# Five due times moved in a two-layer graph attention kernel: a reciprocal and its fetch, one norm, one block turn

## The chip, the cores and the metric

The kernel runs on one core of a Trainium2 chip. The metric is the device time of one execution in microseconds (us). Five engines work beside each other, each through its own instructions in order: TensorE (PE, with its weight loads shown as PEld), VectorE (DVE), ScalarE (ACT), GpSimd (POOL), and SyncE (SP), which here only issues DMAs. POOL also issues some.

## The reference

Two layers of masked attention over 16 graphs of 1024 nodes with 256 features. Layer 0 has 4 heads of 64, layer 1 has 8 heads of 32 and biases. Cut to what matters (the second layer is the same with its own weights):

```python
h = jnp.maximum(_layernorm(x, axis=-1), 0.0)
q, k, v = heads(h @ Wq), heads(h @ Wk), heads(h @ Wv)
scores = q @ k.T * scale                      # per head, 1024 x 1024
scores = jnp.where(adj > 0, scores, -jnp.inf)
out = jax.nn.softmax(scores, axis=-1) @ v
x = x + concat(out) @ Wo.T + bo
```

## The kernel before

**Steps.** `layer_steps` cuts one layer of one batch into groups and steps. A group is one half of the queries (`qh`, 512 of them) with one half of the heads (`g`); each layer has four groups, in the order (qh 0, g 0), (0, 1), (1, 0), (1, 1). A group has 4 steps in layer 0 and 8 in layer 1. A step computes four score tiles of 128 x 512 on TensorE (`scores`, L539) into two pairs of banks out of a ring of three; DVE masks each pair (`exponentials`, L562), which frees its banks; ACT takes the exponential (L568). Two steps later (`LEAD`) `weigh` (L580) multiplies with the values. POOL and accumulating DMAs of POOL's queue (L695, L681) add up the exponentials, and `count` (L425) sums them over the partitions. Layer 0's steps run in pairs, and the scores of a pair need four pairs of banks, one more than the ring has.

**Rounds.** The list of steps alternates: the 16 steps of layer 0 of batch b+1, then the 32 steps of layer 1 of batch b, for b from 0 to 14. This text calls that round b, its layer 0 steps a+0 to a+15 and its layer 1 steps c+0 to c+31 (`a` and `c` in the code). c+32 is a+0 of the next round. Before round 0 stand 16 steps of layer 0 of batch 0, after round 14 the 32 steps of layer 1 of batch 15.

**Due times.** Everything else is written down by hand with `later(i, f, ...)`: at step i, after that step's scores, weighing and exponentials have been issued, call f. Entries of one step run in the order in which they were put down, except that functions with matmuls (`LARGE`) come last. Entries that the program's loop over b puts down (L899 to L944) are there before the first step runs, and so stand ahead of those that `end_group` adds while the steps run. In a pair of layer 0 steps the entries of both follow the exponentials of both; those of the even step come first, then `add_tiles`, then those of the odd one. The instructions go into each engine's queue in this order, which nothing reorders.

**End of a group** (`end_group`, L742). It is called two steps after the group's last step, and puts down, at distances `at`: `spread` (ACT copies the sums out of PSUM, L445; four SP DMAs spread them over the partitions, `sums<-s`, L458), `invert` (a DVE reciprocal, L466, and an SP DMA to DRAM, `vd<-vn`, L468), `fetch` (four SP DMAs that bring it back, repeated over the partitions, `inv<-vd`, L477), `normalize` (POOL, L485), and for g = 1 `end_half` (the product with Wo, L521, and DVE's addition to x, L526). For layer 1 the third group's entry (qh 1, g 0) is `(7, 9, 11, 14)`; the group ends at c+23 and is closed at c+25, so its spread is at c+32 = a+0 of the next round, its invert at a+2, its fetch at a+4 and its normalize at a+7. The fourth group has 4, 6, 7, 9, 11 from c+33: spread at a+5, invert at a+7, fetch at a+8, normalize at a+10, `end_half` at a+12.

**Masks.** `Mask.load` brings a part of adj by four SP DMAs (L152) into one buffer (`bufs=1`); `put` (ACT, L167) rewrites it, `flip` (DVE, L173) turns its blocks, `second` (ACT, L178) changes it for layer 1. In a round the loads of the batch after next stand at a+5, a+8, a+10, a+12, a+14, a+45, a+49 and a+51; the last two are a+1 and a+3 of the next round, and each put stands in the step of the following load, the last one at a+53, which is a+5 of the next round. So at a+5 the put of one batch's last part and the load of the next batch's first part stand in one step.

**Inputs.** `norms` puts down the stats (DVE, L198 and L199, with four small POOL operations) and the norm (ACT, L221, two of them for two row tiles) of half a batch, into one buffer `hn`. `block_inputs` puts down `turn_blocks` (DVE transposes 32 x 32 blocks of hn, L273), `put_blocks` (one SP DMA to DRAM, `turned<-hn`, L278), `place_blocks` (four SP DMAs back as `hT`, L285), and then the matmuls that make k, q and values. In layer 1 of round b that happens for layer 0 of batch b+2 (`other`), and from round 1 on for layer 1 of batch b (`mine`), whose first steps stand at the end of the round before, hence a - 27 and so on. a - 18 is c+14 of the round before.

Of the kernel before, what the change touches and what calls it, by code (L numbers as in the profile page):

```python
# [90 lines left out]
def fast_program(ctx, tc, a, w, loads, chk):  # L91
# [514 lines left out]
    class Stream:  # L606
# [12 lines left out]
        def later(self, i, f, *args):  # L619
            self.due.setdefault(i, []).append((f, args))  # L620
# [121 lines left out]
        def end_group(self, i, gr):  # L742

            if gr.hurry:
                for f in (gr.spread, gr.finish, gr.inp.test):
                    self.later(i, f)
                return

            if gr.layer == 0:
                if gr.g == 0:  # L750
                    gr.half.first = gr
                    return
                early = gr.inp.b == 0 and gr.qh
                self.later(i + (2 if early else 3), gr.count_added)
                at = (3, 4, 5, 7, 13) if gr.qh else (3, 5, 6, 7, 11)
                if gr.inp.b == B - 1 and gr.qh:
                    at = 3, 6, 7, 9, 13
                if gr.inp.b == 0:
                    at = (2, 3, 4, 5, 8) if gr.qh else (3, 5, 6, 7, 9)
            else:  # L760
                at = ((9, 11, 13, 19), (8, 12, 14, 17, 19), (7, 9, 11, 14), None)[2 * gr.qh + gr.g]
                if gr.pairs:
                    at = 2, 5, 6, 7, 9
                elif gr.last:
                    at = 4, 6, 7, 9, 11
            for k, f in zip(at, (gr.spread, gr.invert, gr.fetch, gr.normalize)):
                self.later(i + k, f)
            if gr.last:

                k = 7 if gr.layer or gr.inp.b == 0 else 25 if gr.inp.b == B - 1 else 37  # L770
                self.later(i + k, gr.inp.test)
            if gr.g == 1:
                self.later(i + at[4], gr.end_half)
# [82 lines left out]
    def norms(inp, half, *at, whole=False, bias=None):  # L856

        for k, i in enumerate(at):
            f, rest = (inp.norm, (whole,)) if k > 1 else (inp.stats, ())
            later(i, f, half, (2, 3) if k % 2 else (0, 1), *rest)  # L860
        later(at[3] + 1 if bias is None else bias, inp.add_bias, half)

    def half_inputs(inp, half, *at):

        for i, f in zip(at, (inp.turn, inp.k, inp.q, inp.values)):
            later(i, f, half)

    def block_inputs(inp, half, turn, put, place, *at):

        later(turn, inp.turn_blocks, half)  # L870
        later(put, inp.put_blocks, half)
        later(place, inp.place_blocks, half)
        parts = inp.k_part, inp.q_part, inp.values_part
        for i, f, part in zip(at, (inp.k, inp.q, inp.values), parts):
            if type(i) is tuple:
                for m in range(2):
                    later(i[m], part, half, m)
            else:
                later(i, f, half)
# [19 lines left out]
    for b in range(B - 1):  # L899
        mine, a, c = inputs[1][b], first[b + 1], second[b]  # L900
        if b == 0:

            norms(mine, 0, a + 4, a + 6, a + 7, a + 8, whole=True)
            half_inputs(mine, 0, a + 10, a + 12, a + 13, a + 14)
            norms(mine, 1, a + 10, a + 11, a + 12, a + 13, whole=True)
            half_inputs(mine, 1, a + 15, c, c + 6, c + 2)
        else:
            norms(mine, 0, a - 27, a - 26, a - 19, a - 17, bias=a)
            block_inputs(mine, 0, a - 14, a - 11, a - 5, a, a + 2, a + 8)
            norms(mine, 1, a - 14, a - 14, a - 8, a - 6, bias=a + 6)  # L910
            block_inputs(mine, 1, a, a + 6, a + 7, c, c + (6 if b + 2 < B else 10), c + 2)
        for i, u in zip((0, 2, 4, 6, 7, 9, 11, 13), range(NT)):
            later(a + i, masks[b].second, u)
        if b + 2 < B:
            other, mask = inputs[0][b + 2], masks[b + 2]
            later(a + 6, open_x, b + 2, 0)
            later(c, open_x, b + 2, 1)
            if b == 0:
                norms(other, 0, a + 12, a + 14, c, c + 1, bias=c + 34)
                block_inputs(other, 0, c + 2, c + 3, c + 4, (c + 8, c + 10), (c + 12, c + 16), c + 18)  # L920
                norms(other, 1, c + 3, c + 4, c + 6, c + 7, bias=c + 36)
                block_inputs(other, 1, c + 8, c + 9, c + 12, (c + 20, c + 22), c + 26, (c + 28, c + 30))
            else:
                norms(other, 0, a + 10, a + 12, a + 13, a + 15, bias=c + 34)
                block_inputs(other, 0, c, c + 1, c + 2, (c + 8, c + 10), (c + 12, c + 16), c + 18)
                norms(other, 1, c + 2, c + 4, c + 5, c + 6, bias=c + 36)
                block_inputs(other, 1, c + 7, c + 8, c + 12, (c + 20, c + 22), c + 26, (c + 28, c + 30))
            at = 5, 8, 10, 12, 14, 45, 49, 51, 53
            for t in range(NT):
                later(a + at[t], mask.load, t)  # L930
                later(a + at[t + 1], mask.put, t)
                later(a + at[t + 1] + (1 if t == 4 else 2), mask.flip, t)
        else:
            last, e = inputs[1][b + 1], c + 32
            later(c + 5, last.stats, 0)
            later(c + 10, last.norm, 0)
            later(c + 13, last.add_bias, 0)
            block_inputs(last, 0, c + 11, c + 12, c + 13, c + 18, c + 22, c + 26)
            later(c + 18, last.stats, 1)
            later(c + 22, last.norm, 1)  # L940
            later(c + 23, last.add_bias, 1)
            block_inputs(last, 1, c + 23, c + 24, c + 26, e, e + 10, e + 2)
            for i, u in zip((4, 10, 14, 26, 36, 40, 42, 44), range(NT)):
                later(c + i, masks[b + 1].second, u)  # L944
# [157 lines left out]
def kernel(  # L1102
# [28 lines left out]
    with ExitStack() as fast, tc.manual_schedule():  # L1131
        fast_program(fast, tc, a, w, loads, chk)
# [61 lines left out]
```

## Time and profile before

| what | value |
|---|---|
| median of 3 runs | 3083.88 us (3083.51 to 3085.02) |
| the profiled execution | 3083.88 us |
| its span, first to last instruction | 3082.1 us |
| granted TensorE clock | 0.999 |
| scores L539, on PE | 1089.9 us busy |
| weighing L580, on PE | 967.9 us busy |
| masking L562, on DVE | 1791.6 us busy, 1.215 us each |
| exponentials L568, on ACT | 1615.9 us busy, 1.056 us each |
| tile sums L695, on POOL | 1218.1 us busy, 2.472 us each |
| reciprocal L466, on DVE | 95 of them, 0.244 us each |
| block turn L273, on DVE | 58 of them, 1.239 us each |

Busy times are those of one engine, and the engines overlap. In the timeline, a row is one or several instructions of one line that follow each other: its start in us, its length, engine, line, operation, what it writes and reads, and how many; in brackets stands the idle time of the engine before it and what ended that. SPq rows are DMAs that SP issues: their length is the issuing alone, not the transfer. In the list of waits, a row names who waited for whom, the sum in us, how often, and the longest. An `x8` on a row of scores means the two passes of four matmuls, so one step of layer 1, and `x16` a pair of layer 0 steps.

### The profile page before, as it was taken

To read this page: it belongs to the slowest core of one execution; us is meant where nothing else is said; L and a number is where in the kernel's file an instruction comes from. 1 tells how busy PE (TensorE), PEld (TensorE's weight loads), DVE (VectorE), ACT (ScalarE), POOL (GpSimd) and SP (SyncE) were. 2 spreads that over 40 slices of the span, in tenths; PEclk is the share of its full clock that TensorE was granted. 3 is DMA by queue.
4 is the path that set the end of the run, shared out by engine and by line. 5 is a ranking of instruction groups with operands and counts; after the bars stand their busy time and mean duration, and the time that the engine had idled before them with its cause. 6 is when DMAs were issued, how large, how long until landed. Compare 5 with 4: busy or idle time off the path is not lost.

```text
span 3082.1 us, 46012 instructions
## 1 busy us (share of the span) xinstructions
PE 3061.3 (99%) x16678; PEld 1199.8 (39%) x16678; DVE 2464.4 (80%) x2712; ACT 2242.9 (73%) x2478; POOL 2462.1 (80%) x1584
## 2 busy tenths in 40 slices
PE   9999999999999999999999999999999999999998
PEld 4443433434334343343433334343343433434333
DVE  6778787887878878787887878878788787887877
ACT  5668777777777767777777777777777777776775
POOL 3578788787887878878788887888878778787886
PEclk9999999999999999999999999999999999999999
DMA  4226556464563645546456463654636546463431
GB/s 134 63 61 147 129 123 135 121 141 121 129 145 110 139 130 133 136 110 138 124 129 138 120 139 108 147 123 122 141 104 144 132 122 138 118 143 86 100 82 34
DMA packets 263548, 372.77 MB, mean 121 GB/s; under 512 B 58768, under 2 KB 218768, under 8 KB 242448
## 3 DMA queue, kind: packets, MB, share of 16 engines
q0 software_dynamic: 23472, 170.93, 28.2%
q1 hardware_dynamic: 239520, 198.56, 22.2%
q8 instruction: 133, 2.18, 0.3%
q14 instruction: 103, 0.84, 0.1%
q10 hardware_dynamic: 320, 0.26, 0.0%
HBM read 149.95 MB, written 47.96 MB: 64 GB/s over the span
## 4 chain that ended last, share of the span: by engine, by line
PE 92%; DVE 2%; DMA 2%; POOL 1%; issue 1%; SPq 1%; ACT 1%; DVEq 0%; ACTq 0%; POOLq 0%
PE ps L539 31%; PE po L580 28%; PE pq L307 10%; PE py L521 7%; PE pv L383 6%; PE pq L348 5%; PE pz L425 4%; PE pv L367 2%; DVE p L562 1%; DMA p<-p 1%; POOL p L695 1%; DMA sums<-s 0%; DMA inv<-vd 0%; ACT p L568 0%; SPq L458 0%
## 5 line engine op out<-in xcount | busy, mean ns | idle before, releaser
L562 DVE SCALAR_TENSOR_TENSOR p<-mask,ps 128x1024 f32<-128x1024 fp8e5 x1536 | 1791.6, 1215 | 346.0 <-PE ps L539 327.2
L568 ACT ACTIVATE p<-p 128x1024 f32<-128x1024 f32 x1536 | 1615.9, 1056 | 597.1 <-DVE p L562 535.4
L695 POOL TENSOR_TENSOR p<-p,p 128x1024 f32<-128x1024 f32 x510 | 1218.1, 2472 | 104.9 <-PE po L580 104.3
L539 PE MATMUL ps<-qT,kT 32*128 32x512 f32 (+1 forms) x6144 | 1089.9, 629 | 5.5 <-DVE p L562 3.5
L580 PE MATMUL po<-p,v 128*32 128x512 f32 (+1 forms) x6144 | 967.9, 599 | 0.4 <-ACT cat L437 0.4
L539 PEld LDWEIGHTS ps<-qT,kT 32*128 32x128 f32 (+1 forms) x6144 | 355.4, 184 | 640.2 <-DVE p L562 269.5
L580 PEld LDWEIGHTS po<-p,v 128*32 128x32 f32 (+1 forms) x6144 | 239.4, 118 | 669.7 <-issue 498.6
L593 POOL TENSOR_TENSOR p<-p 128x1024 f32<-128x1024 f32 x128 | 302.8, 2366 | 79.4 <-DVE p L592 74.1
L592 POOL TENSOR_TENSOR p<-p,p 128x1024 f32<-128x1024 f32 x64 | 151.2, 2363 | 157.3 <-DVE p L589 128.9
L485 POOL TENSOR_TENSOR cat<-cat,inv 128x512 f32<-128x512 f32 x127 | 175.2, 1383 | 77.7 <-DMA inv<-vd 76.5
L521 PE MATMUL py<-wo,cat 128*128 128x256 f32 x1008 | 234.4, 386 | 0.0
L521 PEld LDWEIGHTS py<-wo,cat 128*128 128x128 f32 x1008 | 186.3, 190 | 73.5 <-issue 16.7
L681 POOL DMA_DIRECT2D p<-p x163 | 144.8, 889 | 86.5 <-DMA p<-p 55.2
L383 PE MATMUL pv<-wv,hT 128*128 128x256 f32 x800 | 185.7, 385 | 0.0
L307 PE MATMUL pq<-hT,wq 128*128 128x512 f32 x400 | 184.8, 605 | 0.1
L167 ACT ACTIVATE mask<-adj,numbers 128x1024 fp8e5<-128x1024 int32 x128 | 145.9, 1140 | 45.0 <-DMA adj<-in_adj_dram 45.0
L383 PEld LDWEIGHTS pv<-wv,hT 128*128 128x128 f32 x800 | 148.0, 190 | 57.1 <-issue 25.2
L589 DVE TENSOR_TENSOR p<-p 128x1024 f32<-128x1024 f32 x128 | 166.9, 1304 | 0.0
L526 DVE TENSOR_TENSOR x<-py,x 128x1024 f32<-128x1024 f32 x63 | 77.1, 1224 | 109.1 <-PE py L521 109.1
L437 ACT COPY cat<-po 128x512 f32<-128x512 f32 x128 | 73.7, 576 | 118.5 <-PE py L521 96.6
L595 POOL TENSOR_TENSOR p<-p,p 128x1024 f32<-128x1024 f32 x64 | 151.9, 2373 | 5.0
L230 POOL TENSOR_TENSOR x<-x,bo 128x1024 f32<-128x1024 f32 x64 | 155.7, 2503 | 0.0
(71 smaller groups left out, 1961.2 us busy)
## 6 DMA issues: line engine op xcount, KB each, us to landing
p<-p POOLq DMA_DIRECT2D x163, 1024.0 KB, 7.9
adj<-in_adj_dram SPq DMA_DIRECT2D x512, 128.0 KB, 3.0
turned<-hn SPq DMA_DIRECT2D x58, 512.0 KB, 3.6
hT<-turned SPq DMA_DIRECT2D x232, 128.0 KB, 2.9
x<-in_x_dram SPq DMA_DIRECT2D x128, 128.0 KB, 3.0
inv<-vd SPq DMA_DIRECT2D x128, 128.0 KB, 3.0
inv<-vd SPq DMA_DIRECT2D x252, 64.0 KB, 2.5
out_dram<-x SPq DMA_DIRECT2D x124, 128.0 KB, 2.2
```

What stands on the lines that cost most here:

```text
L230: nc.gpsimd.tensor_add(rows, rows, w.bo[self.layer].unsqueeze(1).to_broadcast([P, 4, E]))
L307: nc.tensor.matmul(pq[:, m, :], wt[self.layer][:, c, ts(m, P)], self.hT[half][:, c, :], start=(c == 0), stop=(c == 1),)
L383: nc.tensor.matmul(pv[:, i, :], self.hT[half][:, c, ts(i, P)], w.v[self.layer][:, c, :], start=(c == 0), stop=(c == 1),)
L485: nc.gpsimd.tensor_mul(o, o, inv)
L521: nc.tensor.matmul(py[:, i, :], self.half.cat[:, c, ts(i, P)], w.o[self.layer][:, c, :], start=(c == 0), stop=(c == 1),)
L539: nc.tensor.matmul(st.ps[i // 2][:, i % 2, :], gr.inp.kT[r * D : (r + 1) * D, gr.g, ts(kt, P)], gr.inp.qT[gr.qh][r * D : (r + 1) * D, gr.g ...
L562: nc.vector.scalar_tensor_tensor(out=half, in0=gr.mask.m[gr.qh][:, kt // 4, :, kt % 4].unsqueeze(1).to_broadcast([P, 2, 512]), scalar=-EDG ...
L568: nc.scalar.activation(half, half, AF.Exp, scale=gr.scale)
L580: nc.tensor.matmul(gr.o[r * D : (r + 1) * D, :], gr.inp.v[:, kt, h * D : (h + 1) * D], st.halves[i // 2][:, i % 2, :], start=(kt == 0), st ...
L589: nc.vector.tensor_add(a, a, b)
L593: nc.gpsimd.tensor_add(a, a, b)
L695: nc.gpsimd.tensor_add(half, half, of)
```

## The change

Four lines of due times, in three places. In `end_group`, the third group of layer 1 has its invert two steps later and its fetch one step later. In the loop, the first of the two norms for the first half of the next layer 1 batch is one step later. And the second half of the batch after next has its block turn, its put and its place later: by two, two and one steps in rounds 1 to 13, by one each in round 0.

```diff
             else:
-                at = ((9, 11, 13, 19), (8, 12, 14, 17, 19), (7, 9, 11, 14), None)[2 * gr.qh + gr.g]
+                at = ((9, 11, 13, 19), (8, 12, 14, 17, 19), (7, 11, 12, 14), None)[2 * gr.qh + gr.g]
...
-            norms(mine, 0, a - 27, a - 26, a - 19, a - 17, bias=a)
+            norms(mine, 0, a - 27, a - 26, a - 18, a - 17, bias=a)
...
             if b == 0:
...
                 norms(other, 1, c + 3, c + 4, c + 6, c + 7, bias=c + 36)
-                block_inputs(other, 1, c + 8, c + 9, c + 12, (c + 20, c + 22), c + 26, (c + 28, c + 30))
+                block_inputs(other, 1, c + 9, c + 10, c + 13, (c + 20, c + 22), c + 26, (c + 28, c + 30))
             else:
...
                 norms(other, 1, c + 2, c + 4, c + 5, c + 6, bias=c + 36)
-                block_inputs(other, 1, c + 7, c + 8, c + 12, (c + 20, c + 22), c + 26, (c + 28, c + 30))
+                block_inputs(other, 1, c + 9, c + 10, c + 13, (c + 20, c + 22), c + 26, (c + 28, c + 30))
```

## The prediction

> **What bounds the kernel.** I read the page's busy times first, then the waits, then the timeline of one round, engine by engine. A round is the 48 steps that repeat: the layer 0 pairs a+0 to a+15 of one batch, then the layer 1 steps c+0 to c+31 of the batch before.
>
> ```profile
> PE 3061.3 (99%) x16678; PEld 1199.8 (39%) x16678; DVE 2464.4 (80%) x2712; ACT 2242.9 (73%) x2478; POOL 2462.1 (80%) x1584
> PEclk9999999999999999999999999999999999999999
> PE 92%; DVE 2%; DMA 2%; POOL 1%; issue 1%; SPq 1%; ACT 1%; DVEq 0%; ACTq 0%; POOLq 0%
> DVE vn L466 <- DMA sums<-s: 52.3, 27, 4.4
> ```
>
> TensorE (PE) is busy in all of the span and 92% of the chain that ended last is its own. So a microsecond on another engine counts only where TensorE then stands still. The change moves no matmul: stats, norms, block turns, puts, places, reciprocals and fetches are DVE, ACT, POOL and SP work. TensorE's own work therefore stays, and the answer is the sum of stalls removed and stalls added. I measured them as the distance from one step's first score matmul to the next step's: rounds 1 to 13 lie between 188.76 and 190.38 us, and the shortest time of each of the 48 steps adds up to 188.73. What varies is thus 7.3 us in 13 rounds. A stall that every round has is hidden in those minima; such a one is found by comparing steps with the same work (below, 0.41 us). No large gain exists; losses have no such limit. The last row is the one wait that the reciprocal has: for the sums to land.
>
> **The third group's reciprocal and fetch** (invert from +9 to +11, fetch from +11 to +12 after the group's end). The group ends two steps after c+23, so its spread is at a+0 of the next round, invert goes from a+2 to a+4, fetch from a+4 to a+5, normalize stays at a+7. Removed: in the pair a+2 the reciprocal keeps DVE idle until the sums land (3.27 us in round 5, up to 4.45). After it DVE waits for TensorE anyway ("0.51 <-PE pq L307"), so only the three rounds with the longest waits (7, 8, 9: 4.45, 4.36, 4.17) show TensorE late in a+4 and a+5, by 0.55, 0.46 and 0.45. Gain: **1.5 us**. Added: 0.25 us of DVE in pair a+4, in front of an idle stretch of 2.66 us where DVE waits for the output product; nothing. If that cover were gone it would cost 13 x 0.25 = 3.3.
>
> The fetch is another matter. Entries of one step run in the order in which they were put down, and the round's mask loads are put down before the program runs. In a+5 the order becomes: mask flip, mask put, **mask load, fetch, spread of the fourth group**. The load waits until ACT has read the single adj buffer, and SP is a queue in order:
>
> ```profile
> 1087.48 3.32 SPq L152 DMA_DIRECT2D adj<-in_adj_dram  x4
> 1090.89 1.95 SPq L477 DMA_DIRECT2D inv<-vd  x4
> 1099.84 2.49 SPq L152 DMA_DIRECT2D adj<-in_adj_dram  x4
> 1102.43 2.44 SPq L458 DMA_DIRECT2D sums<-s  x4
> 1104.97 1.99 SPq L529 DMA_DIRECT2D out_dram<-x  x4
> ```
>
> Today (round 5) the third group's fetch (1090.89) runs in the hole before the load at 1099.84, which stands until ACT's put (1098.66 + 1.15) ends. Afterwards it stands between 1102.33 and the fourth group's sums. Its four issues take 1.95 here and 1.91 at the fourth group's fetch (1117.58), the only other row of it with free queues; with the gap to the next issue, **2.0 us**. The sums' four DMAs then go out 2.0 later. What waits for them is the fourth group's reciprocal in a+7, and behind that on DVE stand the mask steps of pair a+8, which free the score banks that TensorE needs:
>
> ```profile
> 1104.98 0.44 DVE L173 STREAM_TRANSPOSE mask<-mask 128x256 f32<-128x256 f32 x1
> 1106.23 0.25 DVE L466 RECIPROCAL vn<-sums 128x16 f32<-128x16 f32 x1 [0.81 <-DMA sums<-s]
> 1106.47 4.62 DVE L562 SCALAR_TENSOR_TENSOR p<-mask,ps 128x1024 f32<-128x1024 fp8e5 x4
> ...
> 2241.74 2.85 PE L539 MATMUL ps<-qT,kT 64*128 64x512 f32 x12
> 2243.64 0.25 DVE L466 RECIPROCAL vn<-sums 128x16 f32<-128x16 f32 x1 [1.78 <-DMA sums<-s]
> 2245.05 1.13 PE L539 MATMUL ps<-qT,kT 64*128 64x512 f32 x4 [0.47 <-DVE p L562]
> ```
>
> Already now the reciprocal stands waiting here, and in round 11 (last three rows) TensorE gets only three of the pair's four score tiles out before DVE is late. Reciprocal start less pair start (r), rounds 1 to 13: 0.93, 1.50, 0.77, 0.74, 0.94, 1.09, 1.20, 0.75, 0.95, 1.57, 1.91, 1.27, 2.14; sum 15.76. TensorE's lateness in a+9 is 0.33, 0.40, 0.74, 0.08 and 0.98 where r is 1.50, 1.57, 1.91, 1.27 and 2.14, plus 0.03 at 1.20, and 0 below: r less 1.17, a slope of one; the sum is 2.56. With 2.0 more every round is over the edge: 15.76 + 13 x (2.0 - 1.17) = 26.6. Added: 26.6 - 2.56 = **24.0 us**. Round 14 has no mask load at a+5 (no batch after the last), and its reciprocal there does not wait: nothing. The bounds: if the landing is not set by the issue, 0; if the four issues go as slowly as the slowest rows of L477 beside other traffic (2.41 at c+6), 13 x 0.4 = 5 more. I take 2.0, from rows with an empty queue like this one. POOL's normalize of this group (1110.01) stays behind the fetch's new landing (last issue near 1104.0, median 2.9 from issue to landing: 1106.9), so it is not late; SP's later outputs and places come 2 us later but TensorE moves by 1.8 too.
>
> The granted clock of the profile is 0.999, with round 13's stall of 0.98 in it; a stall of 1.8 is not in it. The Trainium skill, "TensorE: Matmul & The Clock Gate" (Why this matters for your kernels), says that an idle gap over about 3 us brings the half clock back; 1.8 stays under it. If the clock fell nevertheless, one of that page's windows of 3.4 us at half rate would add an estimated 1.7 a round, 22 in all, and the sum would be near 3123.
>
> **The second half's block turn** (c+7, c+8, c+12 to c+9, c+10, c+13; in round 0 from c+8, c+9, c+12). Here a stall of every round sits:
>
> ```profile
> 1175.84 1.56 PE L539 MATMUL ps<-qT,kT 32*128 32x512 f32 x8
> 1177.27 1.24 DVE L273 STREAM_TRANSPOSE hn<-hn 128x1024 f32<-128x1024 f32 x1
> 1178.43 4.57 DVE L562 SCALAR_TENSOR_TENSOR p<-mask,ps 128x1024 f32<-128x1024 fp8e5 x4
> 1179.24 1.55 PE L539 MATMUL ps<-qT,kT 32*128 32x512 f32 x8
> 1182.58 1.14 PE L539 MATMUL ps<-qT,kT 32*128 32x512 f32 x8
> ...
> 234.69 1.14 PE L539 MATMUL ps<-qT,kT 32*128 32x512 f32 x8
> 234.97 1.24 DVE L273 STREAM_TRANSPOSE hn<-hn 128x1024 f32<-128x1024 f32 x1
> 236.14 2.31 DVE L562 SCALAR_TENSOR_TENSOR p<-mask,ps 128x1024 f32<-128x1024 fp8e5 x2
> ```
>
> The eight score matmuls take 1.14, but 1.56 at c+8 (1175.84) and 1.55 at c+9 (1179.24). At c+8 DVE is late from the q bias (1.38) and stats of c+6, ahead of the turn: that stays. At c+9 it is late by the turn of c+7. Round 0 (last three rows) turns one step later and its c+9 takes 1.14. Moved on two steps, DVE's masks of c+8 follow at once; after c+9's masks (end at its start + 3.51) the turn ends at + 4.67 and the first mask of c+10 at + 5.87, while c+11 starts at + 5.91 (2.92 + 2.99): just clear. Gain 0.41 x 13 = **5.3 us**; bounds 0 (the lateness comes back at c+11) and 5.3. Its DMAs: the put goes out near 1184, the place near 1188 instead of 1182.60, beside POOL's accumulating DMA of 1189; k needs it at c+20 (1216.60), 28 us on. On POOL that next accumulate already waits 2.02; a delay under 2.47 more is swallowed at c+18, where POOL stands idle that long.
>
> **The norm from c+13 to c+14**: two ACT operations of 0.54 each, into the step of 4.72 us with the output product, where ACT has 2.19 of exponentials. Nothing; 13 x 1.08 = 14 if that cover were missing, which these rows exclude.
>
> **The sum**: 24.0 - 1.5 - 5.3 = +17.2. The profiled execution has a span of 3082.1 in 3083.88, which is also the median: 3083.88 + 17.2 = **3101.1**.
>
> **Rivals.** (1) The fetch is hidden: the sums' landing is set by something else than their issue. Then 3083.88 - 6.8 = 3077.1, on the faster side. For it: at a+0 the sums land 7 us after issue, so issue alone does not set landing there. Against: there POOL's accumulating DMAs fill the queues, at a+7 none runs and the reciprocal follows the last issue by 1.4 in most rounds. It decides where the shift is under 0.7 us (stalls then 9.4, gains 6.8). Chance 0.08. (2) The turn's lateness only moves to c+11: 3106.4. The margin of 0.04 speaks for it, round 0 against. Chance 0.15. (3) The shift is 2.4 and the place's traffic delays the accumulate that c+24's sums need (late by 0.67 and 1.11 in rounds 9 and 10) by 0.3 a round: 3101.1 + 5 + 4 = 3110. Chance 0.08. (4) Half a shift, 1.0 us, as the sums' first packets already queue behind mask data: stalls 15.76 - 2.2 = 13.6, so 3083.88 + 11.0 - 6.8 = 3088.1. Chance 0.06. My forecast keeps 0.63, from 3096 to 3106.
>
> The range **3092 to 3109** holds the forecast, (2) and a part of (3). This kernel's measurement tells about 0.2% (6.2 us) from no change: faster 0.06 (most of 1), same 0.07 (the rest of 1, most of 4), slower 0.87.
>
> **What would show it.** Right: in rounds 1 to 13 the SP rows of a+6 read load, inv, sums; the reciprocal of a+8 waits near 2.8 us instead of 0.8; the score matmuls of a+8 break after twelve records by 1.5 to 2.9; the one at a+2 is gone; c+9's eight matmuls take 1.14. Wrong: the reciprocal at a+7 no later than now, or the inv rows still ahead of the load; then the time falls towards 3077.

## The result, and the profile after

The changed kernel takes 3108.78 us (median; 3107.88 to 3113.27), the kernel before 3083.70 beside it: a ratio of 1.0085, 95% interval 1.0071 to 1.0100. The forecast was 3101.1. The direction and the largest term were right; the time lies at the upper edge of the range, some 8 us above the forecast. The profiled execution of after took 3109.21 us with a span of 3107.2, against 3082.1 before, so this one profile has to explain 25.1 us.

The busy times and the chain of the page of after:

```profile
PE 3062.7 (99%) x16678; PEld 1197.7 (39%) x16678; DVE 2470.2 (80%) x2712; ACT 2248.0 (72%) x2478; POOL 2460.4 (79%) x1584
PE 81%; POOL 6%; DVE 5%; issue 3%; DMA 3%; SPq 1%; ACT 1%; DVEq 0%; POOLq 0%; ACTq 0%
```

TensorE's busy time rose by only 1.4 us, so most of the 25 us is time in which it stood still; in the chain its own share fell from 92% to 81%. Four rows of the list of waits (sum, how often, longest) name where:

```profile
PE ps L539 <- DVE p L562: 24.3, 17, 2.4
PE pz L425 <- DMA p<-p: 4.6, 4, 1.7
POOL p L681 <- DMA p<-p: 74.5, 28, 4.6
DVE vn L466 <- DMA sums<-s: 49.0, 28, 3.7
```

Before, they were 3.5 (5 times), 1.4 (2), 55.2 (25) and 52.3 (27). The first is the stall that the prediction spoke of. The second and third are one that its sum did not have (rival 3 named it). The last hardly moved, since what left a+2 came back at a+7.

Step by step, after less before, as distances between first score matmuls, summed over rounds 0 to 14 (+26.6; the stretches ahead of round 0 and behind round 14 are 1.5 shorter in after, which gives the 25.1):

| step | predicted | measured | what |
|---|---|---|---|
| a+9 | +24.0 | +25.8 | masks behind the fourth group's late reciprocal |
| a+4, a+5 | -1.5 | -1.3 | third group's reciprocal gone from a+2 |
| c+9 | -5.3 | -5.4 | block turn gone from c+7, -0.41 in each of 13 rounds |
| c+16 to c+20 | 0 | +3.4 | POOL's chain of accumulates |
| c+24 | 0 | +4.7 | the sums that the count needs |
| c+7, c+8 | 0 | -1.5 | round 14, a half clock in before that after doesn't have |
| all others | 0 | +0.9 | none over 0.7 in size |

**The stall at a+9.** SP's timeline of after in round 5 (the pair a+8 starts at 1110.53):

```profile
1105.08 2.49 SPq L152 DMA_DIRECT2D adj<-in_adj_dram  x4
1107.67 1.92 SPq L477 DMA_DIRECT2D inv<-vd  x4
1109.69 2.44 SPq L458 DMA_DIRECT2D sums<-s  x4
1112.23 1.98 SPq L529 DMA_DIRECT2D out_dram<-x  x4
```

The order is load, fetch, sums, and from the fetch's start to the sums' start it is 2.02. DVE and TensorE in the same stretch:

```profile
1110.22 0.43 DVE L173 STREAM_TRANSPOSE mask<-mask 128x256 f32<-128x256 f32 x1
1110.53 2.85 PE L539 MATMUL ps<-qT,kT 64*128 64x512 f32 x12
1113.48 0.25 DVE L466 RECIPROCAL vn<-sums 128x16 f32<-128x16 f32 x1 [2.83 <-DMA sums<-s]
1113.65 4.57 DVE L562 SCALAR_TENSOR_TENSOR p<-mask,ps 128x1024 f32<-128x1024 fp8e5 x4
1114.89 1.13 PE L539 MATMUL ps<-qT,kT 64*128 64x512 f32 x4 [1.51 <-DVE p L562]
```

DVE has nothing to do for 2.83 us but wait for the sums; three score tiles come out, the fourth has no bank until the first mask has been read.

**The turn.** c+8, c+9 and what follows in round 5 of after, four engines in order of time:

```profile
1182.75 1.56 PE L539 MATMUL ps<-qT,kT 32*128 32x512 f32 x8
1186.16 1.14 PE L539 MATMUL ps<-qT,kT 32*128 32x512 f32 x8
1189.67 1.24 DVE L273 STREAM_TRANSPOSE hn<-hn 128x1024 f32<-128x1024 f32 x1
1190.84 2.31 DVE L562 SCALAR_TENSOR_TENSOR p<-mask,ps 128x1024 f32<-128x1024 fp8e5 x2
1190.94 0.33 SPq L278 DMA_DIRECT2D turned<-hn  x1
1193.58 2.82 SPq L285 DMA_DIRECT2D hT<-turned  x4
1194.37 0.87 POOL L681 DMA_DIRECT2D p<-p  x1
1202.90 0.88 POOL L681 DMA_DIRECT2D p<-p  x1 [2.92 <-DMA p<-p]
```

c+9 takes 1.14 as foretold. But the place now leaves at 1193.58, in the same microseconds as POOL's accumulating DMA of 1194.37, and the next accumulate, which waits for that one to land, leaves 8.53 after it. Before it left 7.64 after it, with the place out of the way:

```profile
1182.60 2.59 SPq L285 DMA_DIRECT2D hT<-turned  x4
1187.57 0.89 POOL L681 DMA_DIRECT2D p<-p  x1
1195.21 0.88 POOL L681 DMA_DIRECT2D p<-p  x1 [2.02 <-DMA p<-p]
```

What this costs is seen in two places. In round 3 DVE's masks wait for a POOL tile sum, and the scores of c+16 take 1.68 instead of 1.14:

```profile
827.09 1.68 PE L539 MATMUL ps<-qT,kT 32*128 32x512 f32 x8
828.68 3.48 DVE L562 SCALAR_TENSOR_TENSOR p<-mask,ps 128x1024 f32<-128x1024 fp8e5 x3 [1.09 <-POOL p L695]
```

The other is 30 us later, at c+24 of round 7:

```profile
1616.54 1.06 PE L580 MATMUL po<-p,v 128*32 128x512 f32 x8
1619.34 0.64 PE L425 MATMUL pz<-p,ones 128*32 128x256 f32 x8 [1.74 <-DMA p<-p]
```

TensorE stands 1.74 us, waiting for the last accumulate of that chain. Four rounds make up most of the loss: 1.94 and 1.90 at c+24 in rounds 7 and 8, 1.31 and 1.42 at c+16 to c+20 in rounds 3 and 10.

### The profile page after: what moved, and what is told of

Read it like the earlier page. It is cut to its first block, busy times and chain, and to the rows that moved or that the text cites. A ratio compares the mean times of both kernels' runs of the same rounds, so it can differ in the third digit from the quotient of the medians.

```text
span 3107.2 us, 45941 instructions
## 1 busy us (share of the span) xinstructions
PE 3062.7 (99%) x16678; PEld 1197.7 (39%) x16678; DVE 2470.2 (80%) x2712; ACT 2248.0 (72%) x2478; POOL 2460.4 (79%) x1584
## 4 chain that ended last, share of the span: by engine, by line
PE 81%; POOL 6%; DVE 5%; issue 3%; DMA 3%; SPq 1%; ACT 1%; DVEq 0%; POOLq 0%; ACTq 0%
PE ps L539 26%; PE po L580 25%; PE pq L307 10%; PE py L521 6%; PE pv L383 6%; PE pq L348 4%; PE pz L425 3%; POOL p L695 3%; DVE p L562 2%; DMA p<-p 2%; PE pv L367 2%; POOL x L230 1%; POOL p L595 1%; POOL p L593 1%; SPq L458 1%
## 5 line engine op out<-in xcount | busy, mean ns | idle before, releaser
L695 POOL TENSOR_TENSOR p<-p,p 128x1024 f32<-128x1024 f32 x510 | 1219.3, 2489 | 98.3 <-PE po L580 97.6
L580 PE MATMUL po<-p,v 128*32 128x512 f32 (+1 forms) x6144 | 970.1, 600 | 0.4 <-ACT cat L437 0.4
L580 PEld LDWEIGHTS po<-p,v 128*32 128x32 f32 (+1 forms) x6144 | 240.1, 118 | 671.7 <-issue 486.7
L681 POOL DMA_DIRECT2D p<-p x163 | 148.3, 910 | 98.8 <-DMA p<-p 74.5
L589 DVE TENSOR_TENSOR p<-p 128x1024 f32<-128x1024 f32 x128 | 177.4, 1386 | 0.0
```

The costliest lines, as they stand in the source:

```text
L580: nc.tensor.matmul(gr.o[r * D : (r + 1) * D, :], gr.inp.v[:, kt, h * D : (h + 1) * D], st.halves[i // 2][:, i % 2, :], start=(kt == 0), st ...
L589: nc.vector.tensor_add(a, a, b)
L695: nc.gpsimd.tensor_add(half, half, of)
```

## The experiments

The theory after the result: the a+9 stall is the fetch ahead of the sums on SP, and the turn gives its 5.4 us back because its later DMAs delay POOL's accumulate. The rivals: the late reciprocal, not the fetch, makes the stall; the turn itself, which DVE now does two steps on, delays POOL's chain. Each ratio is to the kernel before on the same chip.

**Each part alone.** e1 has the turn, put, place and norm of the change, e2 only the third group's entry, e3 the whole change with the fetch one step earlier, which puts it ahead of the mask load, e4 the old reciprocal with the late fetch:

```diff
-    (7, 9, 11, 14)
+    (7, 9, 11, 14)    # e1, with norms and block_inputs of the change
+    (7, 11, 12, 14)   # e2, the rest as before
+    (7, 11, 11, 14)   # e3, with norms and block_inputs of the change
+    (7, 9, 12, 14)    # e4, the rest as before
```

> The block turn, put, place and norm at their new steps, the third group's entry as before (7, 9, 11, 14). Theory A (the whole loss is the third group's fetch behind the mask load; the turn gains 5.3 us at c+9): c+9 gains 0.41 in rounds 1 to 13, a+9 stays as before (2.6 us late in 13 rounds), about 3078. Theory B (the later place runs beside POOL's accumulating DMA and delays the sums that c+24 needs): c+9 gains the same 5.4 and c+16 to c+24 lose some 8 as in the changed kernel: about 3086, no gain at all.

Measured: 3085.36, ratio 1.0006 (0.9996 to 1.0015). c+9 gains 5.4, c+16 to c+20 lose 4.5 and c+24 5.0. The turn is worth nothing as a whole; POOL's wait for accumulates is 75.1 us in sum, as in after.

> Only the third group's invert and fetch later (7, 11, 12, 14); turn, put, place and norm as before. Theory A: a+9 loses 24 to 26 us in 13 rounds, a+4 and a+5 gain 1.3: about 3107. Theory B adds: the c+16 to c+24 loss of the changed kernel is gone, c+24 as before.

Measured: 3107.65, ratio 1.0075 (1.0058 to 1.0092). In its profiled execution (3114.03, span 3112.0) a+9 loses 30.0 and a+4 with a+5 gain 1.3; the clock, below, bears on its excess over the median. Against the expectation c+24 loses 2.4, nearly all in rounds 11 and 12, though the turn stands as before. So c+24 can lose without the turn too; what delays the landing there stays open.

> The changed kernel, but the fetch at +11 as before (7, 11, 11, 14), so that it stands ahead of the mask load on SP though the reciprocal is as late as in the change. Theory A (order on SP): SP rows of a+6 read load, sums; the reciprocal of the fourth group waits 0.6 to 2.0 as before; a+9 back to 2 to 3 us in all; about 3084 (3082 without the second-order loss at c+24). Rival C (the late reciprocal itself delays normalize or DVE): still near 3108.

Measured: 3083.32, ratio 1.0001 (0.9991 to 1.0011). With the fetch ahead of the load nothing is left of the stall (a+9: -1.2), though the reciprocal is as late as in the change; the turn's loss stays (7.4 at c+16 to c+24).

> Only the fetch one step later (7, 9, 12, 14), the reciprocal at its old step. Theory A: the same a+9 loss of 24 to 26 without the gain at a+4 and a+5: about 3109. Rival C: about 3084, as before.

Measured: 3110.54, ratio 1.0087 (1.0070 to 1.0104); a+9 loses 26.9 with the reciprocal where it was. e3 and e4 settle it: the fetch's place in SP's queue is the whole stall, the reciprocal has no part in it.

**Half of the shift.** In e6, e2 with two of the third group's four fetch DMAs issued by ACT:

```diff
+                    third = self.layer and self.qh and not self.g
-                    nc.sync.dma_start(
+                    (nc.scalar if third and r > 1 else nc.sync).dma_start(
```

> Only the third group's entry as in the change (7, 11, 12, 14), but two of its fetch's four DMAs are issued by ACT, so that the fourth group's sums stand behind two fetch issues on SP and not four. Theory A (SP's order, each issue about 0.48 us): the sums go out 1.0 later, a+9 loses 11 us in 13 rounds and not 24 to 30, a+4 and a+5 gain 1.3: about 3093. If the loss came from the fetch's data or from the late reciprocal it would stay near 3108.

Measured: 3094.55, ratio 1.0035 (1.0022 to 1.0048). The timeline of e6 in round 5 (its lines behind L477 are one higher):

```profile
1101.85 2.49 SPq L152 DMA_DIRECT2D adj<-in_adj_dram  x4
1104.44 1.00 SPq L478 DMA_DIRECT2D inv<-vd  x2
1105.53 2.44 SPq L458 DMA_DIRECT2D sums<-s  x4
1109.32 0.25 DVE L466 RECIPROCAL vn<-sums 128x16 f32<-128x16 f32 x1 [1.90 <-DMA sums<-s]
1110.73 1.13 PE L540 MATMUL ps<-qT,kT 64*128 64x512 f32 x4 [0.59 <-DVE p L563]
```

Two issues ahead of the sums hold them 1.09 instead of 2.02, and TensorE's stall falls from 1.51 to 0.59. The sums' landing follows their issue: no shift, half and all of it give +0.0, +11.6 and some +24 us.

**Which part of the turn gives it back.** e5 is the kernel before with the turn one step on instead of two:

```diff
-    block_inputs(other, 1, c + 7, c + 8, c + 12, ...)
+    block_inputs(other, 1, c + 8, c + 9, c + 12, ...)
```

> The third group and the norm as before; the block turn only one step later, at c+8, with its put at c+9 and its place at c+12 (as round 0 has them before the change). Theory B (the loss at c+16 to c+24 comes from the place's data beside POOL's accumulating DMA): the place ends before most of that DMA, POOL's wait at c+13 is near 2.4 us and not 3.1, c+24 loses at most 2 us in all, c+9 gains 5.4: 3079 to 3081. If the loss comes merely from c+9 being earlier while POOL's chain is not, it stays: about 3085.

Measured: 3079.14, ratio 0.9985 (0.9976 to 0.9995). c+9 gains all of its 5.7, and c+16 to c+24 lose only 0.9. One step on is enough for DVE, and the place still leaves 4 us ahead of the accumulate.

**Both repaired.** e7 is e5 with the third group's reciprocal two steps on, its fetch ahead of the load (as in e3), and the fourth group's sums also ahead of it:

```diff
+    (7, 11, 11, 14)
-                    at = 4, 6, 7, 9, 11
+                    at = 4 if gr.brief else 3, 6, 7, 9, 11
```

> As e5_turn_c8, with the third group's invert and fetch both at +11, ahead of the mask load, and the fourth group's spread at +3 (a+4), so that its sums too go out before the mask load. Theory A: the fourth group's reciprocal no longer waits, a+9 loses nothing in any round (2.6 us gained), a+4 and a+5 gain 1.3: 3.9 below e5_turn_c8, 3075 to 3077.

Measured: **3074.99**, ratio 0.9976 (0.9967 to 0.9986), 8 us better than the kernel before, where after was 25 worse. Its round 5:

```profile
1093.51 2.43 SPq L458 DMA_DIRECT2D sums<-s  x4
1097.38 2.51 SPq L152 DMA_DIRECT2D adj<-in_adj_dram  x4
1102.84 3.70 PE L539 MATMUL ps<-qT,kT 64*128 64x512 f32 x16
1102.88 0.21 DVE L466 RECIPROCAL vn<-sums 128x16 f32<-128x16 f32 x1
```

The sums leave 3.87 ahead of the load, the reciprocal waits for nothing, and all sixteen matmuls of the pair run through.

**The other stall of the round.** e8 is e7 with the second pair of stats of `mine` at c+10 instead of c+6, to clear the 0.42 at c+8:

```diff
-            norms(mine, 0, a - 27, a - 26, a - 19, a - 17, bias=a)
+            norms(mine, 0, a - 27, a - 22, a - 19, a - 17, bias=a)
```

> As e7_sums_first, with the second pair of stats for the next layer 1 batch moved from c+6 to c+10, out of the step in which DVE adds the q bias. If DVE's lateness at c+6 is what stretches the score matmuls of c+8 from 1.14 to 1.56 us, c+8 gains 0.42 in 13 rounds: 5.4 below e7_sums_first, about 3071. POOL's four small operations move behind the accumulate of c+9; if that delays the sums of c+24, part of it is lost there.

Measured: 3087.50, ratio 1.0014 (1.0004 to 1.0023). c+8 gains its 5.2, but c+14 loses 19.5; the expectation looked for a loss at c+24. The rows of e8 in round 5:

```profile
1194.96 1.22 DVE L562 SCALAR_TENSOR_TENSOR p<-mask,ps 128x1024 f32<-128x1024 fp8e5 x1 [0.64 <-POOL p L695]
1198.56 3.72 PE L521 MATMUL py<-wo,cat 128*128 128x256 f32 x16 [1.20 <-DVE p L562]
```

The stats come with four small POOL operations, which now stand ahead of a tile sum (L695) whose p buffer DVE's masks are to write into. DVE waits for POOL, TensorE for DVE, and the gain is lost nearly four times over.

**Place or turn.** e5 and e7 moved turn and place together, so the rival that DVE's work delays the chain was still open. Four runs on e7: e9 with the place's due time at c+13, e10 with the turn at c+9 and the place due at c+17, e11 with the turn at c+9 and the place issued by ACT at c+15, e12 as e11 with the turn at c+8:

```diff
-    block_inputs(other, 1, c + 8, c + 9, c + 12, ...)
+    block_inputs(other, 1, c + 8, c + 9, c + 13, ...)     # e9
+    block_inputs(other, 1, c + 9, c + 10, c + 17, ...)    # e10
+    block_inputs(other, 1, c + 9, c + 10, c + 15, ...)    # e11
+    block_inputs(other, 1, c + 8, c + 9, c + 15, ...)     # e12
...
-                nc.sync.dma_start(                            # e11, e12
+                late = half and not self.layer and self.b > 2
+                (nc.scalar if late else nc.sync).dma_start(
```

> The kernel of e7_sums_first with one due time moved: the place of the second half's turned blocks stands at c+13 again, as in the change, while turn and put stay at c+8 and c+9. It asks which of the three steps of the block turn gives its gain back. Theory B (the place's packets beside the accumulating DMA that POOL issues at c+13 let that DMA land later): c+9 keeps its eight matmuls at 1.14 us (-5.3 against before), POOL's wait for the accumulate at c+13 is 2.7 to 3.2 us instead of 1.8, and steps c+16 to c+24 lose 4 to 8 us over the rounds; the time lies 4 to 8 us over e7's 3075.0: 3079 to 3083. Rival A (the turn on DVE at c+9 gives the gain back, the place costs nothing): the turn stands at c+8 here, so the time stays at 3075, within 2 us, with waits of 1.8 at c+13.

> The kernel of e7_sums_first with turn and put at c+9 and c+10, as in the change, and the place at c+17, after the accumulate that POOL waits for has landed and some 6 us ahead of k, which needs it at c+20. Theory B: POOL's wait at c+13 is 1.8 to 2.4 us as before, c+16 to c+24 lose no more than 1 us in all, c+9 gains 5.4: 3074 to 3077, as e7. Rival A: the turn at c+9 pushes DVE's masks of c+9 to c+11 and with them POOL's tile sums, so 5 to 8 us are lost at c+16 to c+24 whatever the place does: 3080 to 3083. A third way: the place lands too late for k, and PE stands at c+20; then c+20 alone loses, and the time can be anything over 3077.

Measured: e9 3075.68, ratio 0.9975 (0.9964 to 0.9986); e10 3081.44, ratio 0.9995 (0.9986 to 1.0005). Taken by the expectations both speak for the rival, but the traces show that neither tested it: the due time doesn't set when the place leaves. SP's and POOL's rows of e10 in round 5:

```profile
1182.17 0.33 SPq L278 DMA_DIRECT2D turned<-hn  x1
1184.81 2.61 SPq L285 DMA_DIRECT2D hT<-turned  x4
1185.72 0.90 POOL L681 DMA_DIRECT2D p<-p  x1
1194.49 0.87 POOL L681 DMA_DIRECT2D p<-p  x1 [3.12 <-DMA p<-p]
```

The place leaves 2.64 after the put, and so it does in round 5 of e7, of e9 and of after, with due times from c+12 to c+17. SP issues nothing else here, so an entry further on in its queue is next anyway, and only the landing of the put holds it. e11 and e12 put the place where something does stand ahead of it, in ACT's queue.

> The kernel of e7_sums_first with turn and put of the second half at c+9 and c+10, as in the change, and from round 1 on the four DMAs of the place issued by ACT at c+15 instead of by SP. On SP the place's due time had no effect: its first issue followed the put's by 2.6 us in e7, e9 and e10 alike, so SP had nothing ahead of it but the put's landing; in ACT's queue it stands behind the exponentials of c+15, some 9 us after the accumulating DMA that POOL waits for at c+13 was issued. Theory B (the place's packets, not the turn on DVE, make that accumulate land later): POOL's wait at c+13 goes back to 1.8 us (2.4 in rounds 1 to 3), the steps c+16 to c+22 lose nothing by it; ACT's four issues cost at most 2 us of its time in a round, ahead of exponentials of c+16 or c+17, where ACT stands idle 2.6 us. Time 3074 to 3079. Rival A (the turn of c+9 itself pushes POOL's chain): the wait stays near 3.0 and the time at 3078 to 3083 and more, as e10's 3076.5 us of span and 3081.4 median.

> e11_place_on_act with turn and put at c+8 and c+9 instead, the place as there. Only the turn and the put differ between the two, so that the cost of the issues on ACT cancels. Theory B: the same as e11 within 1.5 us, waits of 1.8 us at c+13 in both. Rival A: e12 is faster than e11 by 3 us or more, with 1.8 against 3.0 us of wait.

Measured: e11 3077.06, ratio 0.9980 (0.9970 to 0.9990); e12 3076.54, ratio 0.9978 (0.9969 to 0.9988). The rows of e11 in round 5, with the turn as late as in the change:

```profile
1180.43 1.24 DVE L273 STREAM_TRANSPOSE hn<-hn 128x1024 f32<-128x1024 f32 x1
1181.70 0.33 SPq L278 DMA_DIRECT2D turned<-hn  x1
1185.33 0.88 POOL L682 DMA_DIRECT2D p<-p  x1
1192.75 0.88 POOL L682 DMA_DIRECT2D p<-p  x1 [1.80 <-DMA p<-p]
1200.02 4.81 ACTq L286 DMA_DIRECT2D hT<-turned  x4
```

The accumulate's successor leaves 7.42 after it, against 8.77 in e10 with the same turn. e11 and e12 lie 0.5 us apart. So it is the place's DMAs, by when they run. Only the runs that shift the place late show it in the accumulate that leaves near 44.9: from its issue to its landing it takes 8.0 to 8.3 us (medians) in the four with the place at 44.1, and 6.9 in all others. In e11 and e12 the next but one, which leaves at 58.4, takes 8.1 to 8.2 instead of 6.9 to 7.4, and nothing waits for it at once. e11 changes the place's queue and its time together; no run parts the two.

All runs by when the place's first DMA leaves (us after c+0, median of the rounds), the sum of POOL's waits for accumulates in the list of waits, and what the steps c+16 to c+20 and c+24 lose against before:

| run | turn | place leaves | POOL's waits | loss |
|---|---|---|---|---|
| before | c+7 | 40.0 | 55.2 | 0 |
| e4 | c+7 | 40.1 | 55.8 | 0.4 |
| e6 | c+7 | 40.0 | 57.3 | 1.6 |
| e2 | c+7 | 40.0 | 58.3 | 2.5 |
| e8 | c+8 | 40.7 | 34.9 | -0.1 |
| e5 | c+8 | 41.0 | 46.7 | 0.9 |
| e7 | c+8 | 41.0 | 53.6 | 0.8 |
| e9 | c+8 | 41.0 | 53.1 | 1.0 |
| e12 | c+8 | 59.8, by ACT | 53.7 | 0.7 |
| e11 | c+9 | 59.8, by ACT | 52.6 | 1.6 |
| e10 | c+9 | 44.1 | 74.5 | 4.2 |
| e3 | c+9 | 44.1 | 74.6 | 7.4 |
| after | c+9 | 44.1 | 74.5 | 8.1 |
| e1 | c+9 | 44.1 | 75.1 | 9.5 |

The accumulate leaves at about 44.9 in all of them. The turn at c+9 costs 20 us of POOL's waiting with the place at 44.1 and nothing with it at 59.8. What TensorE loses by it varies, from 4.2 to 9.5 us in these profiles, and e2 comes up to 2.5 without it; e10's profiled execution, the fastest of its ten, was 3 us under its median. The medians, each less that of the kernel before beside it, are clearer: the late place costs 5.3 us (e10 less e11), 6.8 (e10 less e7) and 5.8 (e1 less e5).

## Why the prediction was right in sign and too low

**The fetch behind the load: right.** The order, the 2.0 of shift (2.02 in round 5, 1.09 with half of it) and the stall came as foretold. Round for round it fits where nothing else happened: rounds 1, 3, 4, 5, 8 and 9 were to lose 1.76, 1.60, 1.57, 1.77, 1.58 and 1.78 and lost 1.77, 1.64, 1.58, 1.78, 1.58 and 1.79. Rounds 2, 6, 7 and 13 lost less (1.35, 1.68, 1.62 and 1.28 for 1.9 to 2.0), rounds 10 to 12 more (3.90, 3.40, 2.48), and two of these for a reason of their own, the clock, next. In round 13 the sums left only 1.29 later, as they had been late before; in round 12 they left 3.01 later. Rival 1, the hidden fetch, and rival 4, half a shift, are out by the SP rows; e6 shows that rival 4's sum (3088.1 with the turn's gain, so 3093.4 without it) was right for half a shift.

**The clock: half right.** The prediction let the page's rule of an idle gap over about 3 us stand and kept the full clock. In round 10 of after the stall is 2.38, and the clock fell:

```profile
2072.12 1.21 PE L539 MATMUL ps<-qT,kT 64*128 64x512 f32 x4 [2.38 <-DVE p L562]
2073.26 5.22 PE L580 MATMUL po<-p,v 128*64 128x512 f32 x16
```

Sixteen matmuls of L580 take 3.65 at full clock. The windows of that stretch (length, busy us of PE, PEld, DVE, ACT and POOL, then the granted clock, the DMA share, GB/s):

```profile
2069.62:2073.04 3.42, 1.04 (x6) 0.30 (x4) 2.32 (x3) 0.94 (x1) 3.33 (x3) 1.00 0.63 174
2073.04:2076.45 3.41, 3.41 (x10) 1.00 (x10) 3.41 (x4) 3.13 (x4) 2.81 (x8) 0.50 0.81 281
```

The half clock holds for 3.41 us and costs 1.57. It happened in rounds 10 and 11: 3.2 of the 25.8 us. Without it a+9 lost 22.6 for a predicted 24.0; e2 had four such windows (some 6.4 of its 30.0) and e4 two (3.2 of 26.9), which leaves 23.6 and 23.7. So the term itself was sized well, and the price of 1.7 that the prediction set on a window was close; that only stalls over 3 us bring one was wrong. The profile of before spoke against it already: it has a half clock window at 2878.44, in round 14, after a stall of 1.23 (last section). After lacks that one, which gives 1.5 back at c+7 and c+8.

**The reciprocal: right**, 1.3 for 1.5, in rounds 7 to 9 as named. **The norm: right**, nothing. c+14 is up by 0.3, but in e2 and e5, whose norm stands as before, it is as well.

**The block turn: wrong as a whole.** Its gain at c+9 was exact, and rival 2 (the lateness moves to c+11) didn't come about: the margin of 0.04 held. The step that failed is the next one, "a delay under 2.47 more is swallowed at c+18, where POOL stands idle that long". POOL waits only 0.7 to 1.3 us longer for the accumulate at c+13, in twelve of thirteen rounds, well under 2.47, and still 8.1 us came back at c+16 to c+24.

POOL itself does make it up: in round 7 the accumulate at c+18 leaves at 69.65 after c+0 (69.41 before) and the last at 78.86 (78.95). But the delay reaches TensorE by two ways that don't lead over POOL's idle time. Ahead of c+18, DVE's masks wait for POOL's tile sums, as in round 3 above (before, DVE waited there for TensorE, 0.23); c+16 to c+20 lose 3.4, of which 2.7 in rounds 3 and 10. And at c+24 the count waits for a landing, which TensorE, freed at c+9, asks for 0.41 earlier. In round 7, in us after c+0: the last accumulate leaves at 78.95 before, 78.86 in after and 78.55 in e7; it lands at 87.15, 89.26 and 86.95 (semaphore records); the count could start at 87.8, 87.4 and 87.4, and started at 87.8, 89.4 and 87.4. There was half a microsecond of slack, not 2.47. From issue to landing that accumulate took 8.20, 10.39 and 8.39; a load of instructions (last section) holds one of its packets in after's rounds 7 and 8, and what else stretches it there no run shows apart.

Rival 3 named this mechanism and its place, but priced it at 0.3 a round, 4 in all, and gave it a chance of 0.08. That its sum, 3110, lies near the result is luck: 5 us of it stood for a shift of 2.4, and the shift was 2.0.

So the miss of 7.9 us in the profile (25.1 for 17.2) is: the accumulate +8.1, the half clock at a+9 +3.2 and the one missing in round 14 -1.5, the rest of a+9 -1.4, and -0.5 in small steps and at the two ends; the accumulate alone would have moved the forecast to 3109.2.

## What to carry to other kernels

A move that frees an engine also moves the DMAs that follow from it: ask beside which transfers they will run, and follow the one that is hit to its last reader, not to the first idle time behind it. A due time sets an order in a queue, not a time; where the queue is empty it sets nothing, and to hold a transfer back something has to stand ahead of it. In a queue in order the transfer with the nearest reader belongs first: here fetch, load, sums (e3) instead of load, fetch, sums (after) is worth some 25 us with the same transfers, and fetch, sums, load (e7) takes the last 2.6 off a+9.

## What the hardware showed that was not expected

**The clock falls by windows, not by the length of a stall.** In after, e2 and e4 the half-clock stretches begin at whole multiples of 3.413 us from each other (57.00 and 114.00 of them, for instance) and last 3.41, once 6.83. Cut along that grid, and without the end of the program, each of the seven windows of these three traces with 1.94 us or more of idle TensorE was followed by half clock, and those with 1.26 to 1.77 were not; one exception is round 14's c+7, where 1.23 was enough in several executions, of before too:

```profile
2875.03:2878.44 3.41, 2.18 (x12) 0.59 (x16) 3.31 (x7) 1.07 (x2) 3.11 (x4) 1.00 0.00 0
2878.44:2881.85 3.41, 3.41 (x17) 0.64 (x16) 2.38 (x3) 3.16 (x3) 3.33 (x4) 0.50 1.06 219
```

In e2 the half clock of 2069.48 went on for a second window after only 0.6 of idle time. So idle time alone isn't the whole measure; what sets these two cases apart stays open. Two stalls in after of 2.29 and 1.99, and the longest of e4, 2.84, fell across an edge of the grid and cost nothing more. So the same stall costs 1.6 more or not by where the window falls, which fits that the profiled execution of e2, with four such windows, lies 6 us above its median. The Trainium skill, "TensorE: Matmul & The Clock Gate" (What's actually happening), says that the window is free-running and 3413 ns long, which these runs show; its limit of about 3 us (Why this matters for your kernels) is too high here.

**Small packets run in between large ones.** In round 5 of after the packet records show the place's 512-byte packets in between the accumulate's 8192-byte ones, which take some 0.63 each. The Trainium skill, "DMA: Bandwidth & Descriptors" (Queues, rings and completion order), says that each DMA engine goes round its queues packet by packet, which agrees. The accumulate landed 7.99 after its issue, against 7.10 before, and the next accumulate, which waits for that, left 0.9 later. At c+24 of rounds 7 and 8 one 16 KB load of instructions on one of the sixteen DMA engines, 0.93 to 0.97 us long, came in front of the accumulate's last packet there, which so started 1.3 to 1.4 after those of the fifteen others; before, the load stood just behind it. With it a small lateness of the chain (0.1 and 0.2 us at the count in rounds 5 and 6) became a stall of 1.74.

**An issue on SP isn't always the same.** Four DMAs of the sums take 2.44 in round 5 and 3.24 in round 10 of after, with the same work around them, and 3.19 in round 10 of before; the reason stays open.
